# A square root moved ahead of ScalarE's loads, a convolution's first loads moved to GpSimd's queue, and a last store cut in three

## Chip, cores and metric

The kernel runs on one core of a Trainium2 chip. The metric is the device time of one execution in microseconds (us); the time of a kernel is the median of several executions. The engines are named as the profile names them: PE is TensorE, DVE is VectorE, ACT is ScalarE, POOL is GpSimd and SP is SyncE, which here only issues transfers. ACT and POOL issue transfers too, between their computing instructions.

## What is computed

Input `x` is one image of 384 channels and 192 x 192 pixels in float32. Two residual layers follow each other:

```
x = x + attention(gn(x))     # 1x1 conv to q,k,v; 2x2 max pool; 3x3 depthwise conv;
                             # 8 heads of channel attention with four top-k softmaxes;
                             # gelu; 2x2 repeat; 1x1 conv
x = x + conv(gn(x))          # seven depthwise convs (13x13 and six smaller, dilated ones),
                             # each with a batch norm, summed
```

`gn` is a group norm over 32 groups of 12 channels. The seven depthwise convolutions are merged into one of 13 x 13 taps per channel: each set of taps is multiplied by its batch norm's scale, `gamma * rsqrt(var + 1e-5)`, and the sets are added. The batch norms' shifts sum to one value per channel, `shift`.

## The kernel before

Channels stand in 3 tiles of 128 partitions (`NJ` = 3). The kernel has five stages, and within each the order of each engine's instructions is the order in which the Python code issues them (`manual_schedule`), so an engine or a queue that waits holds up all that was issued behind it on the same engine.

**Statistics of x.** Four tiles `xt` (1152 KB each, loaded by SP, line 162) hold the first 16 image rows, and 66 blocks `xs` (768 KB each, line 204) hold the rest. Blocks with an even number are loaded by SP, the others by ACT; ten buffers rotate. `load_block` is called for ten blocks first (lines 207, 208). Then `rsqrt` (lines 86 to 104) computes the scale of the taps: DVE adds eps, ACT takes the square root (line 95), DVE refines it. Lines 210 to 214 make `scale` and `shift` on DVE; POOL scales the taps (lines 216 to 227) and stores them as `wfd`. Behind these on DVE stand 24 `bn_stats` over the `xt` tiles (lines 232, 233) and 198 over the `xs` blocks (line 238), with one `bn_aggr` after each third (line 242). Each pass over a block frees its buffer and so lets the load ten blocks later be issued. `group_stats` (line 106) then turns the channels' mean and variance into those of the groups through tiny matmuls, and the result is `gn0`.

**Projection, pooling and depthwise convolution** (line 339 on PE, 350 and 386 on DVE), then **attention applied to v** (line 709).

**Projection out** (lines 1009 to 1070). A loop over 72 steps, n = 0 to 71, `NBB` = 24 for each channel tile. A step is six matmuls `pj` on PE (line 1018, three of 128 x 128 weights, each executed in two passes), an ACT pass that writes `pjs` (line 1026), a DVE pass that adds the pixel sums `smj` to get `cell` (line 1033), `bn_stats` on DVE (line 1034) and a store of `pjs` to the buffer `pd` in HBM by ACT's queue (line 1036). `load_sum` loads `smj` on SP's queue four steps ahead (line 1005). Three PSUM buffers lie between PE and the two readers. Beside it, generators in the list `running` are advanced once a step:

- `derive(i, ...)` starts at steps 24 and 48 and after the loop. It computes the second group norm's statistics from the channel tiles known so far, through `group_stats`, whose matmuls stand between the steps' matmuls on PE; POOL copies `sv` for it (line 817).
- `load_rows(0)` starts at step 28 (`NBB + 4`) and `load_rows(1)` at step 46. Each loads for the four row phases `u` a piece `raw` of x (line 873) and a piece `up` of `pd` (line 880) on SP's queue, one `u` a step. `load_rows(0)` has ten transfers, `load_rows(1)` eight. `up` can't be loaded before `pd` is stored.
- `load_taps(0)` at step 33 loads 1536 KB of taps `wt` on SP's queue (line 893).
- `residual(0)` on POOL (line 910) from step 37, then at step 44 `patch(0)` on DVE and three passes `normalize1(0, q)` on ACT (line 918), and the transposes `arrange(0, 1)` on DVE (line 933) in two of three steps after it. They prepare the convolution's first chunk.

In the built program every SP or ACT load and store also waits for the transfer eight before it among those of SP and ACT together: their completion is counted on eight shared counters. POOL's transfers have eight counters of their own.

**Convolution** (lines 1081 to 1107). 48 chunks of 8 channels, each 8 times 5 matmuls (line 949), an ACT pass to `co` (line 957), and one chunk later `finish`: one DVE transpose from `co` to `o` (line 963) and four stores to `out`, one for each `u`, by POOL's queue (line 972). `finish` of the last chunk stands alone at the end.

Of the kernel before, what the change touches and what calls it, by code (L numbers as in the profile page):

```python
# [7 lines left out]
F32 = mybir.dt.float32  # L8
AF = mybir.ActivationFunctionType
ALU = mybir.AluOpType  # L10
# [4 lines left out]
P = 128  # L15
C = 384
NJ = C // P
H = W = 192
HW = H * W
# [13 lines left out]
UQ = 4  # L33
# [27 lines left out]
def tile_attn_then_large_kernel_conv(ctx: ExitStack, tc: tile.TileContext, a: dict, out: bass.AP):  # L61
# [43 lines left out]

    def group_stats(pool, psum, mv, name):


        ps = psum.tile([NG, 1], F32, tag="gs", name=f"{name}_ps")
        for j in range(NJ):  # L110
            nc.tensor.matmul(ps, lhsT=gm[:, j, :], rhs=mv[:, j, 0:1], start=(j == 0), stop=(j == NJ - 1))  # L111
        mean = pool.tile([NG, 1], F32, name=f"{name}_mean")
        nc.vector.tensor_copy(mean, ps)
        yield
        yield

        pb = psum.tile([P, NJ, 1], F32, tag="gs", name=f"{name}_pb")
        for j in range(NJ):
            nc.tensor.matmul(pb[:, j], lhsT=gmt[:, j * P : (j + 1) * P], rhs=mean, start=True, stop=True)
        s = pool.tile([P, NJ, 1], F32, name=f"{name}_s")  # L120
        nc.vector.tensor_sub(s, mv[:, :, 0:1], pb)
        nc.vector.tensor_mul(s, s, s)
        nc.vector.tensor_add(s, s, mv[:, :, 1:2])
        yield
        yield
        pv = psum.tile([NG, 1], F32, tag="gs", name=f"{name}_pv")
        for j in range(NJ):
            nc.tensor.matmul(pv, lhsT=gm[:, j, :], rhs=s[:, j], start=(j == 0), stop=(j == NJ - 1))
        var = pool.tile([NG, 1], F32, name=f"{name}_var")
        nc.vector.tensor_copy(var, pv)  # L130
        r = rsqrt(pool, var, 1e-5, name)
        sb = pool.tile([NG, 2], F32, name=f"{name}_sb")
        nc.vector.tensor_copy(sb[:, 0:1], r)
        nc.vector.scalar_tensor_tensor(sb[:, 1:2], mean, -1.0, r, ALU.mult, ALU.mult)
        yield
        yield
        pc = psum.tile([P, NJ, 2], F32, tag="gs", name=f"{name}_pc")
        for j in range(NJ):
            nc.tensor.matmul(pc[:, j], lhsT=gmt[:, j * P : (j + 1) * P], rhs=sb, start=True, stop=True)
        return pc  # L140
# [29 lines left out]
    with (  # L170
# [35 lines left out]

        for n in range(10):
            load_block(n)
        scale = rsqrt(s1, bn[:, :, 3, :], 1e-5, "bn")
# [3 lines left out]
        nc.vector.tensor_sub(sh, bn[:, :, 1, :], sh)  # L213
        nc.vector.tensor_reduce(shift, sh, AX.X, ALU.add)
        c0 = BC - 1
        for j in range(NJ):
# [34 lines left out]
    with ExitStack() as ctx_v:  # L251
# [537 lines left out]
        def derive(i, stats):  # L789
# [6 lines left out]
            yield  # L796
            pc = yield from group_stats(d1, d_ps, mv1, f"g1_{i}")
            chp = d1.tile([P, NJ, 2], F32, name="chp", tag="chp")
            nc.vector.tensor_copy(chp, pc)

            sd = d1.tile([P, NJ], F32, name="sd", tag="sd")
            nc.vector.reciprocal(sd, chp[:, :, 0])
            mean = d1.tile([P, NJ], F32, name="mean", tag="mean")
            nc.vector.tensor_mul(mean, chp[:, :, 1], sd)
            nc.vector.tensor_sub(mean, shift, mean)
            yield
            j0 = max(0, i - 1)
            nj = i + 1 - j0
            dd = d1.tile([P, KK, nj * 2], F32, name="dd", tag="dd")
            nc.vector.tensor_mul(  # L810
                dd,
                of.unsqueeze(2).to_broadcast([P, KK, nj * 2]),
                chp[:, j0 : i + 1].rearrange("p j s -> p (j s)").unsqueeze(1).to_broadcast([P, KK, nj * 2]),
            )
            sv = d1.tile([P, 2, nj, P], F32, name="sv", tag="sv")
            for q, t in enumerate((mean, sd)):
                nc.gpsimd.tensor_copy(sv[:, q], t[:, j0 : i + 1].unsqueeze(2).to_broadcast([P, nj, P]))
            yield
# [10 lines left out]
            ps = d_ps.tile([P, 2, nj, P], F32, tag="gs", name=f"shp{i}")  # L829
            nc.vector.tensor_copy(par[:, :, j0 : i + 1], pp.rearrange("p k (j s) -> p k j s", s=2))  # L830
            for q in range(2):
                nc.vector.tensor_scalar(
                    edge[:, q, :, j0 : i + 1], par[:, :, j0 : i + 1], inside[:, q : q + 1], None, ALU.mult
                )
# [16 lines left out]

        def load_rows(k):
            raw = raws[k] = rotate("raw", k, max(0, k - 1), [P, ME + 1, W], 3)
# [8 lines left out]
            for u in range(UQ):  # L862
# [9 lines left out]
                for p0, p1, m0, m1 in parts:  # L872
                    nc.sync.dma_start(
                        out=raw[u * 32 + p0 : u * 32 + p1, m0:m1],
                        in_=bass.AP(
                            x.tensor, o + p0 * rows + m0 * UQ * W, [[rows, p1 - p0], [UQ * W, m1 - m0], [1, W]]
                        ),
                    )
                par_u, back = (1, 1) if u < 2 else (0, 0)
                nc.sync.dma_start(  # L880
                    out=up[u * 32 : (u + 1) * 32].rearrange("p m w -> p (m w)"),
# [7 lines left out]

        def load_taps(k):  # L890
            wt = taps[k] = rotate("wt", k, k, [P, CC, ZS], 3)
            j, kk = divmod(k, KK)
            nc.sync.dma_start(out=wt, in_=zds[j][kk * CC : (kk + 1) * CC].rearrange("c p z -> p c z"))

# [63 lines left out]

        def finish(k, co, lo):

            o = lo.tile([P, TE, 2, W], F32, tag="o", name=f"o_{k}")
            at, of = o[:, 0], co[:, :, 0, :]
            nc.vector.transpose(  # L963
                bass.AP(at.tensor, at.offset, [list(at.ap[0]), [2 * W, TE], [BC, NBQ], [W, 2], [1, BC]]),
                bass.AP(
                    of.tensor,
                    of.offset,
                    [list(of.ap[0]), [NBQ, TE], [1, NBQ], [NT * NBQ, CC], [TE * NBQ, NE]],
                ),
            )  # L970
            for u in range(UQ):
                nc.gpsimd.dma_start(  # L972
                    out=bass.AP(
                        out.tensor,
                        out.offset + k * CC * HW + 2 * u * W,
                        [[ME * UQ * W, CC * NE], [BR * W, TE], [1, 2 * W]],
                    ),
                    in_=o[u * 32 : (u + 1) * 32].rearrange("p t y w -> p t (y w)"),
                )

        def all_of(gen):
# [12 lines left out]
        with (  # L994
# [4 lines left out]
            with tc.manual_schedule():  # L999
# [9 lines left out]
                for n in range(NJ * NBB):  # L1009
# [34 lines left out]
                    if n == NBB + 4:  # L1044
                        running.append(load_rows(0))
                    if n == NBB + 9:
                        load_taps(0)
                    if n == NBB + 13:
# [10 lines left out]
                    if n == NBB + 22:  # L1059
                        running.append(load_rows(1))  # L1060
                    if n == 2 * NBB + 12:
# [12 lines left out]
    with (  # L1074
# [5 lines left out]
        with tc.manual_schedule():  # L1080
# [4 lines left out]
            for k in range(NK):  # L1085
# [20 lines left out]
                last = co  # L1106
            finish(NK - 1, last, lo)
    ctx_l1.close()
# [49 lines left out]
```

## Time and profile before

| | |
|---|---|
| median of 5 executions | 3181.41 us (3180.43 to 3183.49) |
| profiled execution: its own time | 3181.41 us |
| its span, from first to last instruction | 3179.3 us |
| around the span | 2.1 us |
| PE busy | 2982.9 us (94%) |
| DVE busy | 2488.9 us (78%) |
| ACT busy | 1228.2 us (39%) |
| POOL busy | 869.0 us (27%) |

| stage | from | to |
|---|---|---|
| statistics of x | 0 | 172.4 |
| projection, pooling, attention | 172.4 | 2065.5 |
| projection out | 2065.5 | 2227.5 |
| convolution | 2227.5 | 3164.9 |
| last transpose and stores | 3164.9 | 3179.3 |

The bounds of the stages are starts of instructions in the timeline, in us from the span's start. A busy share over the whole span says little here, as the stages have different limits.

### The profile page before, as it was taken

The page shows a single profiled execution, that of the slowest core. Times are in us where ns is not written, and L with a number is a line of the kernel's source. Part 1 is how long each engine was busy: PE and PEld are TensorE (multiplying, and loading weights), DVE is VectorE, ACT ScalarE, POOL GpSimd, SP SyncE. Part 2 cuts the span into 40 slices and gives each one's busy share as a digit, 9 for nine tenths or more (in the row PEclk, how much of TensorE's full clock was granted, in tenths as well). Part 3 has the DMA queues.
Part 4 walks back from the last instruction along what each step waited for, and adds up shares of the span by engine and source line. Part 5 has one row for each costly group of instructions (what it writes and reads, how often), then busy time and mean ns, then how long its engine had stood idle before and what let it go on. Part 6 is the DMA issues. An engine that isn't in the chain of part 4 may idle for free.

```text
span 3179.3 us, 31595 instructions
## 1 busy us (share of the span) xinstructions
PE 2982.9 (94%) x10978; PEld 1972.0 (62%) x10978; DVE 2488.9 (78%) x3385; ACT 1228.2 (39%) x2288; POOL 869.0 (27%) x1026
## 2 busy tenths in 40 slices
PE   0089999999999999999999999998999999999998
PEld 0056666666666666665555555555777777777776
DVE  6967887878778787879999998356788777777775
ACT  0034444444444444444444443332333333333332
POOL 3023232332323233222222221001333333333332
PEclk9999999999999999999999999999999999999999
DMA  9924444343444434333333333366999999999984
GB/s 371 385 79 121 121 126 124 109 119 110 118 129 122 118 113 116 113 102 125 100 98 114 112 101 113 117 198 208 256 251 249 239 244 240 243 244 240 242 214 107
DMA packets 277744, 528.65 MB, mean 166 GB/s; under 512 B 22132, under 2 KB 193088, under 8 KB 277584
## 3 DMA queue, kind: packets, MB, share of 16 engines
q1 hardware_dynamic: 208064, 338.72, 39.3%
q0 software_dynamic: 43728, 147.74, 16.8%
q10 hardware_dynamic: 25792, 40.17, 3.4%
q8 instruction: 86, 1.41, 0.2%
q14 instruction: 74, 0.61, 0.1%
HBM read 365.18 MB, written 161.37 MB: 166 GB/s over the span
## 4 chain that ended last, share of the span: by engine, by line
PE 87%; DVE 9%; DMA 2%; issue 0%; ACT 0%; POOL 0%; SPq 0%; ACTq 0%; POOLq 0%; DVEq 0%
PE qkv L339 48%; PE conv L949 29%; PE pj L1018 4%; DVE stats L238 4%; PE av L709 3%; DVE v L386 3%; PE gram L427 2%; PE tr L415 2%; DVE mx L350 1%; DMA xt<-in_x 1%; DMA smj<-sums 0%; DMA up<-pd 0%; DMA wt<-zd 0%; DMA pd<-pjs 0%; DVE stats L232 0%
## 5 line engine op out<-in xcount | busy, mean ns | idle before, releaser
L339 PE MATMUL qkv<-xt,wqk 128*128 128x384 f32 x3456 | 1132.8, 487 | 1.3 <-ACT xt L316 1.3
L949 PE MATMUL conv<-xp,wt 128*128 128x288 f32 x3840 | 933.1, 406 | 1.1 <-ACT co L957 1.1
L339 PEld LDWEIGHTS qkv<-xt,wqk 128*128 128x128 f32 x3456 | 650.4, 190 | 435.8 <-ACT xt L316 2.1
L949 PEld LDWEIGHTS conv<-xp,wt 128*128 128x128 f32 x3840 | 729.0, 190 | 202.7 <-ACT co L957 1.6
L386 DVE SCALAR_TENSOR_TENSOR acc<-pooled,wd,acc 128x384 f32<-128x384 f32 (+2 forms) x1152 | 721.0, 626 | 30.6
L350 DVE TENSOR_REDUCE mx<-qkv 128x192 f32<-128x768 f32 x432 | 412.9, 956 | 252.8 <-PE qkv L339 240.6
L933 DVE STREAM_TRANSPOSE xp<-xn 128x4608 f32<-128x4608 f32 (+1 forms) x107 | 442.0, 4131 | 194.5 <-PE conv L949 175.2
L357 ACT ACTIVATE pooled<-mx,bq 128x192 f32<-128x192 f32 x432 | 196.8, 455 | 963.5 <-DVE mx L350 963.5
L339 PE MATMUL qkv<-xt,wv 128*128 128x384 f32 x1728 | 563.4, 487 | 1.6 <-ACT xt L316 1.1
L339 PEld LDWEIGHTS qkv<-xt,wv 128*128 128x128 f32 x1728 | 325.6, 190 | 234.4 <-ACT xt L316 7.1
L957 ACT ACTIVATE co<-conv,cb 128x288 f32<-128x288 f32 x384 | 191.3, 498 | 604.8 <-PE conv L949 604.7
L386 DVE SCALAR_TENSOR_TENSOR v<-pooled,wd,v 128x384 f32<-128x384 f32 (+2 forms) x576 | 375.6, 652 | 15.2
L316 ACT ACTIVATE xt<-xt,gn 128x768 f32<-128x768 f32 x288 | 284.8, 1013 | 2.9 <-DVE gn L243 2.9
L324 POOL TENSOR_TENSOR sum<-xt 128x192 f32<-128x192 f32 x144 | 94.6, 657 | 699.6 <-ACT xt L316 699.0
L972 POOL DMA_DIRECT2D out<-o x192 | 107.3, 594 | 580.5 <-DVE o L963 527.2
L910 POOL TENSOR_TENSOR raw<-raw,up 128x2496 f32<-128x2496 f32 (+2 forms) x56 | 242.5, 4336 | 40.2 <-DMA up<-pd 25.8
L963 DVE STREAM_TRANSPOSE o<-co 128x2304 f32<-128x2304 f32 x48 | 209.8, 4370 | 20.5 <-ACT co L957 20.5
L455 POOL DMA_DIRECT2D zd<-v x96 | 72.0, 756 | 510.7 <-ACT v L446 510.7
L111 PE MATMUL g_ps<-mv,gm 128*32 128x1 f32 x24 | 2.0, 182 | 164.8 <-DVE mv L242 164.2
L1018 PE MATMUL pj<-v,wp 128*128 128x384 f32 x432 | 148.2, 502 | 6.4 <-DVE cell L1033 5.9
L1018 PEld LDWEIGHTS pj<-v,wp 128*128 128x128 f32 x432 | 83.1, 195 | 64.6 <-DVE cell L1033 8.3
L1033 DVE SCALAR_TENSOR_TENSOR cell<-smj,quarter,pj 128x384 f32<-128x384 f32 x72 | 43.8, 608 | 100.3 <-ACT pjs L1026 83.5
(162 smaller groups left out, 1808.5 us busy)
## 6 DMA issues: line engine op xcount, KB each, us to landing
xt<-in_x SPq DMA_DIRECT2D x96, 1152.0 KB, 5.5
wt<-zd SPq DMA_DIRECT2D x48, 1536.0 KB, 13.5
raw<-in_x SPq DMA_DIRECT2D x188, 312.0 KB, 12.5
out<-o POOLq DMA_DIRECT2D x192, 288.0 KB, 6.0
zd<-v POOLq DMA_DIRECT2D x96, 416.0 KB, 4.9
up<-pd SPq DMA_DIRECT2D x192, 156.0 KB, 11.8
xs<-in_x ACTq DMA_DIRECT2D x33, 768.0 KB, 9.6
xs<-in_x SPq DMA_DIRECT2D x33, 768.0 KB, 10.7
```

The source lines that it names most:

```text
L238: nc.vector.bn_stats(stats[:, j, NS0 + b * (FB // 512) + q, :], xt[:, q * 512 : (q + 1) * 512])
L316: nc.scalar.activation(xt[:, j], xt[:, j], AF.Identity, bias=gn0[:, j, 1:2], scale=gn0[:, j, 0:1])
L339: nc.tensor.matmul(ps[:, r, : 2 * W], lhsT=wq[:, j, mm * P : (mm + 1) * P], rhs=xt[:, j, r * 2 * W : (r + 1) * 2 * W], start=(j == 0), sto ...
L350: nc.vector.tensor_reduce(mx, ps[:, :, : 2 * W].rearrange("p r (y w x) -> p r w y x", y=2, x=2), AX.XY, ALU.max,)
L357: nc.scalar.activation(pool_t[m][:, k : k + SR, 1 : 1 + WS], mx, AF.Identity, bias=bq[:, m : m + 1])
L386: nc.vector.scalar_tensor_tensor(acc[:, :nt], pool_t[m][:, k0 + dy : k0 + dy + nt, dx : dx + WS], wd[:, m, t : t + 1], acc[:, :nt], ALU.mu ...
L910: nc.gpsimd.tensor_add(rv, rv, uv.unsqueeze(2).to_broadcast([P, (m1 - m0) * WS, 2]))
L933: nc.vector.transpose(bass.AP(at.tensor, at.offset, [list(at.ap[0]), [NBQ, n], [1, NBQ], [NQ * NBQ, CC], [ME * NBQ, NE]],), bass.AP(row.te ...
L949: nc.tensor.matmul(ps, lhsT=wt[:, c, o : o + P], rhs=d[:, c, g : g + 2 * NT - 1 : 2, :], start=(g == 0), stop=(g == NGR - 1),)
L957: nc.scalar.activation(co[:, c], ps, AF.Identity, bias=cb[:, cc : cc + 1])
L963: nc.vector.transpose(bass.AP(at.tensor, at.offset, [list(at.ap[0]), [2 * W, TE], [BC, NBQ], [W, 2], [1, BC]]), bass.AP(of.tensor, of.offs ...
L1018: nc.tensor.matmul(ps, lhsT=wp[:, j, i * P : (i + 1) * P], rhs=v[:, j, b * RB : (b + 1) * RB, :].rearrange("p r w -> p (r w)"), start=(j = ...
```

## The change

Four edits:

- The calls of `load_block` for the first ten blocks move from ahead of `rsqrt` to behind line 214. On ACT the square root now stands ahead of its first `xs` load. In the built program POOL's nine clearing passes over the pooling tiles (line 303) move in among the scaling of the taps, and on SP the loads `wqk`, `wv` and `bpj` move back among the `xs` loads.
- `load_rows(0)`, `load_taps(0)` and `load_rows(1)` issue their 19 transfers on POOL's queue instead of SP's. In the built program `load_rows(0)` and `load_rows(1)` stand on POOL ahead of the `sv` copies of `derive(0)` and `derive(1)`, the taps between `sv` and `residual(0)`; SP is left with the `smj` loads alone in that loop.
- `group_stats` takes the channel tiles to work on. `derive(i)` passes `range(i + 1)` instead of all three, so it has one tile's matmuls in each of its four groups for i = 0, two for i = 1, three for i = 2; its later small DVE passes cover only the tiles that are used.
- `finish` of the last chunk works in three pieces of two of the six row groups each: three transposes, and after each one four stores, issued by SP, ACT, POOL and SP.

```diff
-    def group_stats(pool, psum, mv, name):
+    def group_stats(pool, psum, mv, name, js=range(NJ)):
+        own = slice(js[0], js[-1] + 1)
...
-        for j in range(NJ):
+        for j in js:
...
-        for n in range(10):
-            load_block(n)
         scale = rsqrt(s1, bn[:, :, 3, :], 1e-5, "bn")
         nc.vector.tensor_mul(scale, scale, bn[:, :, 0, :])
         sh = s1.tile([P, NJ, 7], F32, name="sh")
         nc.vector.tensor_mul(sh, bn[:, :, 2, :], scale)
         nc.vector.tensor_sub(sh, bn[:, :, 1, :], sh)
         nc.vector.tensor_reduce(shift, sh, AX.X, ALU.add)
+        for n in range(10):
+            load_block(n)
...
-            pc = yield from group_stats(d1, d_ps, mv1, f"g1_{i}")
+            pc = yield from group_stats(d1, d_ps, mv1, f"g1_{i}", range(i + 1))
...
-        def load_rows(k):
+        def load_rows(k, eng=nc.sync):
...
-                    nc.sync.dma_start(
+                    eng.dma_start(
...
-        def load_taps(k):
+        def load_taps(k, eng=nc.sync):
...
-        def finish(k, co, lo):
+        def finish(k, co, lo, n=TE, engines=(nc.gpsimd,)):
             o = lo.tile([P, TE, 2, W], F32, tag="o", name=f"o_{k}")
+            for t0 in range(0, TE, n):
+                at, of = o[:, t0], co[:, :, t0, :]
+                nc.vector.transpose(...)
+                for u in range(UQ):
+                    engines[u % len(engines)].dma_start(...)
...
-                        running.append(load_rows(0))
+                        running.append(load_rows(0, nc.gpsimd))
                     if n == NBB + 9:
-                        load_taps(0)
+                        load_taps(0, nc.gpsimd)
...
-                        running.append(load_rows(1))
+                        running.append(load_rows(1, nc.gpsimd))
...
-            finish(NK - 1, last, lo)
+            finish(NK - 1, last, lo, 2, (nc.sync, nc.scalar, nc.gpsimd, nc.sync))
```

## The prediction

> **What bounds the kernel now.** I read the page first, then the chain of waits by stage, then the timeline and the table by stretches at the three places that the change touches. The page's chain says that PE carries most of the end, with DVE and some DMA between:
>
> ```profile
> span 3179.3 us, 31595 instructions
> PE 87%; DVE 9%; DMA 2%; issue 0%; ACT 0%; POOL 0%; SPq 0%; ACTq 0%; POOLq 0%; DVEq 0%
> ```
>
> The change touches no matmul of PE's two long stages, so what can move lies where PE does not carry: the head, the projection out and the tail.
>
> The head, from the timeline (start, duration, engine, line, operation; in brackets the idle time before and what ended it):
>
> ```profile
> 4.82 0.18 DVE L91 TENSOR_SCALAR bn_ve<-bn 128x21 f32<-128x21 f32 x1 [3.94 <-DMA bn<-in_bn]
> ...
> 27.37 0.22 ACT L95 ACTIVATE bn_sd<-bn_ve 128x21 f32<-128x21 f32 x1
> 27.62 0.29 DVE L97 RECIPROCAL bn_r<-bn_sd 128x21 f32<-128x21 f32 x1 [22.62 <-ACT bn_sd L95]
> ...
> 162.48 2.16 DVE L242 BATCH_NORM_AGGREGATE mv<-stats 128x2 f32<-128x444 f32 x1
> ```
>
> The input of the square root is ready at 5.0 and ACT takes it at 27.4, behind five load issues that last 22.55 us. DVE sits for 22.62 us with all the statistics queued behind the reciprocal. From 29.55, its first statistics, to 164.64 it runs without a gap: PE's group matmuls, then the projection, wait for that. The table by stretches (start:end length, busy time of each engine, granted clock, DMA share, GB/s) shows the second limit:
>
> ```profile
> 25.00:40.00 15.00, 0.00 (x0) 0.00 (x0) 12.10 (x32) 1.50 (x2) 9.74 (x30) 1.00 1.02 413
> 40.00:50.00 10.00, 0.00 (x0) 0.00 (x0) 10.00 (x18) 0.00 (x0) 3.21 (x11) 1.00 0.89 293
> 50.00:150.00 100.00, 0.54 (x4) 0.37 (x4) 99.93 (x165) 0.00 (x0) 0.00 (x0) 1.00 1.02 416
> 150.00:153.10 3.10, 0.00 (x0) 0.00 (x0) 3.10 (x6) 0.00 (x0) 0.00 (x0) 1.00 0.96 393
> 153.10:164.70 11.60, 0.01 (x1) 0.01 (x1) 11.50 (x17) 0.00 (x0) 0.00 (x0) 1.00 0.01 5
> ```
>
> Transfers run at 416 GB/s nearly throughout and end at 153.1, with a dip at 40 to 50 when all ten buffers were full. So DVE can't win its whole 22 us: the loads are next.
>
> The projection out, in the chain:
>
> ```profile
> 2141.07 5.09 DMA pd<-pjs
> 2147.16 7.54 DMA smj<-sums
> 2155.50 9.71 PE pj L1018 x24
> 2166.49 1.90 DMA smj<-sums
> 2187.88 2.23 DMA pd<-pjs
> 2190.17 4.21 DMA smj<-sums
> ```
>
> Loads of `smj` stand behind `raw`, `up` and `wt` on SP's queue, which wait for stores of `pd`; then `cell` is late, the PSUM buffers stay full and PE stops. PE was busy 153.2 of the 162.0 us from 2065.5 to 2227.5.
>
> The tail, in the timeline:
>
> ```profile
> 3164.86 4.31 DVE L963 STREAM_TRANSPOSE o<-co 128x2304 f32<-128x2304 f32 x1 [15.05 <-ACT co L957]
> 3169.46 2.24 POOL L972 DMA_DIRECT2D out<-o x4 [17.12 <-DVE o L963]
> ```
>
> The table by stretches has the packets of these stores at 3170.5 to 3176.2, 207 GB/s, and nothing from there to the end at 3179.3.
>
> **The square root first.** On ACT it now waits only for `bn_ve` (5.0): done at 5.3, and DVE's chain behind it (27.62 to 29.6, 2.0 us) ends at 7.3. The first `xt`, issued at 2.2, lands 5.8 us later, at 8.0, so the cover of that chain is the load itself. ACT's first `xs` goes out at about 5.5 instead of 3.5; four `xt` are in transit meanwhile (DMA share 1.00 from 4 to 10), so I cost it at nothing, and at most 2.0 us. POOL's clearing passes move into its scaling work, which ended at 43 and now ends near 30; its result is next read at 171. `wqk` and `wv` (1.73 MB) go out later, still far ahead of the first matmul.
>
> DVE's own bound: the last `xt` lands by 3.7 + 17.2 = 20.9; the first `xs` by 4.6 + 22.5 = 27.1 (22.5 is the longest of these landings). From there 198 x 0.593 + 3 x 2.16 = 123.9 us, so 151.0. The loads' bound: the bytes are the same, and the dip is gone, (416 - 293) x 10 / 416 = 3.0 us, so they end at 150.1 instead of 153.1. Behind the last landing come one or two blocks (1.78 us each) and the last aggregate, 2.16: 154.0 to 155.8. This is later than 151.0, so the loads decide. The aggregate ended at 164.64: gain 8.8 to 10.6, less 2.0 if ACT's later start counts, and less some 3 us if the two queues, now fed in another order, leave gaps like that of 40 to 50. I take 9.5, and 5 to 10.6 as ends. The group matmuls and the 1893 us that follow just move forward.
>
> A rule of the Trainium skill speaks against this. SBUF — State Buffer, section "SBUF: two separate sides", gives HBM to one core about 358 GB/s and calls HBM almost always the bottleneck. By that the 60 MB of the head could not land before 168 us and the gain would be nothing; the rows above, 416 GB/s over 100 us, contradict it, and I go by them.
>
> **Loads on POOL's queue.** What goes: in 2065.5 to 2227.5 PE was idle 8.8 us, and all but pieces of it hangs on late `smj` (2147 to 2155 alone has 8.4 us for 6 matmuls, which take 2.03 elsewhere). SP is left with `smj`, four steps or 8 us ahead of use, landing in 2.5 us. What is late next: at step 44 ACT has three more passes (3.2 us) and DVE eight (1.7 us), and at step 54 DVE has ten small passes of `derive(1)` beside `cell`, `bn_stats` and a transpose, some 4 us in a step of 2.03. The three PSUM buffers absorb about two steps; I leave 1.5 us of idle time, between 0.5 and 5.
>
> What comes: 19 issues on POOL. The trace has no such load on this queue. The nearest rows are its stores: `zd` in many small pieces 0.76 us an issue and 4.9 to landing, the clearing stores 1.70 and up to 13.0, `out` 0.58 and 6.0. POOL is nearly idle in this stage (11 us of 162), so 19 x 0.76 = 14 us or 19 x 1.70 = 32 us costs POOL nothing. What waits behind: `sv` (step 32, its matmuls some five steps later), then `residual(0)`, whose result ACT needs at step 44, about 2157. The stores of the first tile's `pd` end near 2117.5. Ten transfers, two in turn because the ninth and tenth wait for earlier ones: 2117.5 + 6 + 2 x 6 = 2136 by the small rows, 2117.5 + 12 + 2 x 13 = 2156 by the clearing rows. The taps follow `sv` at 2133 and land at 2141 to 2148. `residual(0)` takes 5.5 us: done at 2142 to 2161. Cost 0, or 4 us at the far end. I take 0, as sizes and pieces are closest to `zd`.
>
> [...]
>
> **Fewer group matmuls.** These stand on PE between the steps. The four groups of `derive(0)` took 0.28, 0.75, 0.28 and 0.76 us; two thirds go: 1.4. Of `derive(1)` one third: 0.7. The small DVE passes shrink from 3 columns to 1 or 2; 128x3 takes 0.16 and 32x1 0.15, so nothing. Together 2.1 us, if PE carries the stage, which it does.
>
> The stage: 8.8 - 1.5 + 2.1 = 9.4 us gained; ends 2 (5 us of idle time and 4 late rows, with only part of the rest) and 10.9. The start of the convolution (a wait for `wt` and `up` of later chunks, PE idle 1.2 us) keeps its loads on SP and I leave it.
>
> **The tail.** Three transposes of 768 elements, 4.31 / 3 = 1.44 each: ready at 3166.3, 3167.8, 3169.2. The last piece is 0.39 MB instead of 1.18. POOL's first packets came 1.04 us after its issue started, so at 3170.5 as before; 0.39 MB at 207 GB/s is 1.9 us, so packets end at 3172.4, and with the same 3.1 us after them the span ends at 3175.5: gain 3.8. If the earlier pieces' 0.79 MB from 3167.4 on is still in the way, 3173.1: gain 3.1. At the 416 GB/s of the head: 4.8.
>
> **The sum**, against the profiled execution, 3181.41, of which 2.1 lie around the span; it equals the median: 9.5 + 9.4 + 3.8 = 22.7, so 3158.7.
>
> **Rivals.**
> The first: in the head the loads' new order leaves gaps, or two queues with eight transfers in flight don't hold 416 GB/s from the start. For it: 324 GB/s in the first 25 us. Against: 413 as soon as ten blocks are queued. Gain 4 instead of 9.5: 3164.2.
> The second: the projection out stays short of PE's pace, because DVE's work around steps 44 to 60 was as much the cause as `smj`. For it: 2.1 us of PE's idle time is put down to `dd` on DVE. Against: DVE was behind there because of `smj`. Gain 3 instead of 9.4: 3165.1. Both together: 3170.6.
> The third ends slower: `raw`, `up` or `wt` come so late through POOL's queue that `patch(0)` and `normalize1(0)`, issued at step 44, hold up every later `cell` and `pjs` behind them on DVE and ACT. It decides once they are over 22.7 us later than 2157; at 45 us late, 3181.4 - 22.7 + 45 = 3203.7. Against: it takes landings of over 20 us, where this queue's longest is 13.0.
> That an edit does nothing is not open: the built order has each of them.
>
> **How the numbers follow.** All three gains, 0.72: 3158.7, by the ends of the terms 3154 to 3165. First rival 0.08, second 0.12, both 0.03, third 0.03; 0.02 for what I don't see. The range that leaves out 2 in 10 at most runs from 3154 (10.6 + 10.9 + 4.8 = 26.3 gives 3155.1, and a microsecond of spread) to 3168. Runs of this kernel lie within 0.1% of their median, so about 0.2%, 6.4 us, can be told from no change: faster 0.94, the same 0.03, slower 0.03.
>
> **What would show it.** Right: `bn_sd` on ACT near 5; the first statistics near 8; gaps on DVE between `xs` blocks, ended by DMA; the last aggregate at 154 to 157; DMA near 416 from 25 to 150. `smj` not in the chain; PE busy 151 of about 152.6 us in the projection out; POOL's load issues under 1 us. Three transposes of 1.4 us and the end 6 us behind the last. Wrong: an aggregate later than 160, PE waits for `cell` or ACT's `xn` after step 44, `raw` on POOL waiting for DMA past 2150 (less the head's gain), or packets in the tail past 3173.

## The result, and the profile after

The changed kernel takes 3174.57 us (median of 21 executions, 3171.07 to 3176.21); the kernel before, run beside it, takes 3180.97 us (41 executions, 3178.34 to 3184.44). The ratio is 0.9978, with a 95% interval of 0.9972 to 0.9984: faster by 6.4 us. The forecast was 3158.7 us, 22.7 us faster, with a range from 3154 to 3168. The sign was right; the size was not, and the time lies outside the range.

The profiled execution took 3172.44 us, 2.1 us less than its median. In its page's chain of waits PE has 86% instead of 87%, DVE 8% instead of 9%, and DMA 4% instead of 2%.

Stage by stage, in us, each stage bounded by the starts of the same instructions in both timelines:

| stage | forecast gain | before | after | gain |
|---|---|---|---|---|
| statistics of x, to the first `qkv` | 9.5 | 172.37 | 167.07 | 5.3 |
| projection, pooling, attention, to the first `pj` | 0 | 1893.11 | 1892.79 | 0.3 |
| projection out, to the first `conv` | 9.4 | 162.05 | 160.71 | 1.3 |
| convolution, to the last transpose | 0 | 937.33 | 938.19 | -0.9 |
| last transpose to the end of the span | 3.8 | 14.4 | 11.8 | 2.6 |

Before rounding the gains add up to the 8.7 us by which the span is shorter. All three terms are gains, and two of them are smaller than forecast, by some 4 and 8 us. The 1.3 us of the projection out are less than the 2 us by which this stage differs between executions (see the experiments).

**The head**, in the timeline (start, duration, engine, line, operation; in brackets the idle time before it and what ended it):

```profile
5.17 0.22 ACT L95 ACTIVATE bn_sd<-bn_ve 128x21 f32<-128x21 f32 x1 [1.37 <-DVE bn_ve L91]
...
7.90 0.69 DVE L233 BATCH_NORM_STATS2 stats<-xt 128x6 f32<-128x512 f32 x1 [0.47 <-DMA xt<-in_x]
...
70.64 1.88 DVE L239 BATCH_NORM_STATS2 stats<-xs 128x6 f32<-128x512 f32 x3 [5.14 <-DMA xs<-in_x]
...
157.17 2.16 DVE L243 BATCH_NORM_AGGREGATE mv<-stats 128x2 f32<-128x444 f32 x1
```

The square root ran at 5.17 instead of 27.37 and the first statistics at 7.90 instead of 29.55, as forecast. But DVE, which ran without a gap before, now stands still for 5.14 us in the middle of the loads, and the last aggregate ends at 159.33 instead of 164.64. The table by stretches (start:end length, busy time of each engine, granted clock, DMA share, GB/s) shows that the DMA did not stand still with it:

```profile
40.00:50.00 10.00, 0.00 (x0) 0.00 (x0) 9.10 (x16) 0.00 (x0) 0.00 (x0) 1.00 1.02 417
...
65.00:71.00 6.00, 0.00 (x0) 0.00 (x0) 0.86 (x2) 0.00 (x0) 0.00 (x0) 1.00 1.02 415
71.00:150.00 79.00, 0.54 (x4) 0.36 (x4) 78.80 (x129) 0.00 (x0) 0.00 (x0) 1.00 1.02 414
150.00:153.00 3.00, 0.00 (x0) 0.00 (x0) 3.00 (x7) 0.00 (x0) 0.00 (x0) 1.00 0.12 49
```

The dip of 40 to 50 us is gone (417 GB/s instead of 293), the transfers end near 150 as forecast, and at 65 to 71 they run at 415 GB/s while DVE has 0.86 us of work in 6. What they carry there is in the chain of waits (start, duration, what):

```profile
33.33 17.18 DMA xs<-in_x
...
50.52 18.22 DMA wqk<-in_wqkvT
...
68.81 14.86 DMA xs<-in_x
```

The weights `wqk` and `wv` (1152 and 576 KB) were issued at 29.00 and 29.42 before, when DVE was behind and the buffers were full:

```profile
29.00 0.38 SPq L272 DMA_DIRECT2D wqk<-in_wqkvT  x1
```

They are issued at 50.52 and 58.52 now, among the blocks that DVE is waiting for; and the `xs` load that shares its counter with `wqk` is not issued before `wqk` has landed, at 68.8.

**The projection out**, in the table of waits between 2059 and 2221 (who waited for whom: us in total, times, longest):

```profile
ACT pjs L1030 <- DMA pd<-pjs: 15.8, 5, 5.5
...
PE pp L823 <- DVE dd L812: 2.8, 1, 2.8
...
DVE cell L1037 <- DMA smj<-sums: 2.8, 2, 1.5
```

The same table of the kernel before, between 2065.5 and 2227.5, has

```profile
DVE cell L1033 <- DMA smj<-sums: 16.6, 6, 5.1
...
ACT pjs L1026 <- DMA pd<-pjs: 4.7, 2, 2.8
```

`smj`, which `cell` waited 16.6 us for, is down to 2.8 us. In its place ACT waits 15.8 us, where it waited 4.7, for stores of its own: `pjs` has three buffers, and a store of `pd` that is late leaves ACT without one. The chain of this stage has the two late stores, and a third piece that is new:

```profile
2113.37 8.04 DMA pd<-pjs
...
2130.71 5.27 DVE dd L812
...
2166.81 12.60 DMA pd<-pjs
```

The time from issue to landing of the stores of `pd`, where the trace has the landing, in the kernel before and in the changed one:

```profile
DMA to landing us min/median/max: 2.0/2.1/7.4
...
DMA to landing us min/median/max: 2.0/2.1/12.6
```

Each of the two late ones was issued within a burst of eight loads on POOL (2109.88 to 2114.4 and 2162.98 to 2167.7), which issues them at about 0.6 us each as soon as nothing holds it. The timeline of POOL and DVE:

```profile
2109.88 0.52 POOL L882 DMA_DIRECT2D up<-pd  x1 [158.33 <-DMA pd<-pjs]
...
2130.58 5.39 DVE L812 TENSOR_TENSOR dd<-of,chp 128x32 f32<-128x32 f32 x1
2130.95 5.46 POOL L912 TENSOR_TENSOR raw<-raw,up 128x576 f32<-128x576 f32 x5
```

The last two rows belong to the piece with `dd`. This DVE pass of `derive(0)` took 0.17 us in the kernel before and takes 5.39 us here, beside the five adds of `residual(0)` on POOL; it ends at 2135.97, just behind the fourth add (2135.91). PE waits 2.8 us for the `dd` that feeds its `pp`. The `dd` of `derive(1)` starts 0.2 us behind the first add of `residual(1)` and takes 1.14 us in both kernels: it waits for that one add.

**The tail**, in the timeline:

```profile
3158.76 4.42 DVE L967 STREAM_TRANSPOSE o<-co 128x768 f32<-128x768 f32 x3 [15.05 <-ACT co L959]
```

Three transposes as forecast, with the stores of each behind it on three engines; the last packets move at 3166.2, 7.4 us behind the start of the transposes, where the forecast had 7.5. The end of the span comes another 4.4 us later, where it had 3.1.

### The profile page after: what moved, and what is told of

The parts are those of the page before. It is cut to its first block, busy times and chain, and to the rows that moved or that the text cites. A ratio compares the mean times of both kernels' runs of the same rounds, so it can differ in the third digit from the quotient of the medians.

```text
span 3170.6 us, 31552 instructions
## 1 busy us (share of the span) xinstructions
PE 2979.6 (94%) x10954; PEld 1969.4 (62%) x10954; DVE 2498.3 (79%) x3387; ACT 1228.1 (39%) x2288; POOL 878.4 (28%) x1044
## 4 chain that ended last, share of the span: by engine, by line
PE 86%; DVE 8%; DMA 4%; issue 1%; POOL 0%; ACT 0%; SPq 0%; DVEq 0%; POOLq 0%; ACTq 0%
PE qkv L340 48%; PE conv L951 28%; PE av L710 3%; PE pj L1022 3%; DVE v L387 3%; DVE stats L239 2%; PE gram L428 2%; PE tr L416 2%; DVE mx L351 1%; DMA xs<-in_x 1%; DMA xt<-in_x 1%; DMA pd<-pjs 1%; DMA wqk<-in_wqkvT 1%; DMA raw<-in_x 1%; DVE cell L1037 0%
## 5 line engine op out<-in xcount | busy, mean ns | idle before, releaser
L967 DVE STREAM_TRANSPOSE o<-co 128x2304 f32<-128x2304 f32 (+1 forms) x50 | 209.9, 4202 | 20.5 <-ACT co L959 20.5
L1022 PE MATMUL pj<-v,wp 128*128 128x384 f32 x432 | 146.2, 498 | 2.5 <-DVE cell L1037 1.9
L239 DVE BATCH_NORM_STATS2 stats<-xs 128x6 f32<-128x512 f32 x198 | 118.4, 677 | 6.6 <-DMA xs<-in_x 5.9
## 6 DMA issues: line engine op xcount, KB each, us to landing
wt<-zd SPq DMA_DIRECT2D x47, 1536.0 KB, 12.6
raw<-in_x SPq DMA_DIRECT2D x182, 312.0 KB, 12.5
xs<-in_x ACTq DMA_DIRECT2D x33, 768.0 KB, 12.1
```

The lines of the kernel that those rows point to most:

```text
L239: nc.vector.bn_stats(stats[:, j, NS0 + b * (FB // 512) + q, :], xt[:, q * 512 : (q + 1) * 512])
L967: nc.vector.transpose(bass.AP(at.tensor, at.offset, [list(at.ap[0]), [2 * W, n], [BC, NBQ], [W, 2], [1, BC]]), bass.AP(of.tensor, of.offse ...
L1022: nc.tensor.matmul(ps, lhsT=wp[:, j, i * P : (i + 1) * P], rhs=v[:, j, b * RB : (b + 1) * RB, :].rearrange("p r w -> p (r w)"), start=(j = ...
```

## The experiments

The theory after the comparison: (1) the head lost what the moved weights take, since from 28 us on DVE takes a block in 1.88 us on average, the aggregates counted in (123.9 us for 66 blocks), and the loads bring one in 1.89 (768 KB at 416 GB/s), so that DVE never makes up a gap; (2) the projection out lost its gain to stores of `pd` that land late beside POOL's loads and to too few buffers behind them, and to `dd` beside POOL's adds. The rivals: in the head, that two queues simply go less well together; in the projection out, that PE's matmuls or DVE were the bound anyway, so that the queue had nothing to give. All ratios are to the kernel before, run beside each, with 95% intervals; differences to the changed kernel are between medians of separate runs, and by the ratios they come out the same within 2 us. Stages of one execution vary: kernels with the same code in the projection out (before, the square root alone, the tail alone) had 162.05, 162.18 and 164.23 us there, so differences of 2 us in one profile mean nothing.

### Each edit alone

**The square root alone**, on the kernel before:

```diff
-        for n in range(10):
-            load_block(n)
         scale = rsqrt(s1, bn[:, :, 3, :], 1e-5, "bn")
...
+        for n in range(10):
+            load_block(n)
```

> The kernel before with the first edit alone: the ten calls of load_block behind the square root. If the head of the changed kernel is this edit's work alone, the last aggregate ends at 159.3 as there (164.6 before), with DVE waiting 5 us near 65 to 71 behind the load of wqk, and the time falls by 5.3 us (ratio 0.9983). If the trace's head was only a lucky execution, the time falls by less than 3 us (ratio above 0.999).

3175.46 us, ratio 0.9980 [0.9971, 0.9989]. PE starts `qkv` at 166.91, against 167.07 with all edits. The gap on DVE, in the timeline, is there to the tenth:

```profile
70.57 3.66 DVE L238 BATCH_NORM_STATS2 stats<-xs 128x6 f32<-128x512 f32 x6 [5.20 <-DMA xs<-in_x]
```

So the whole gain of the head is this edit's, and its shortfall too.

**POOL's queue alone**, on the kernel before:

```diff
-                        running.append(load_rows(0))
+                        running.append(load_rows(0, nc.gpsimd))
-                        load_taps(0)
+                        load_taps(0, nc.gpsimd)
-                        running.append(load_rows(1))
+                        running.append(load_rows(1, nc.gpsimd))
```

> The kernel before with the second edit alone: load_rows(0), load_taps(0) and load_rows(1) on POOL's queue. Theory: POOL has nothing that paces it, issues the transfers in one burst, the stores of pd land after 8 us and more instead of 2, ACT runs out of its three pjs buffers and PE stops; the projection out gains 0 to 2 us of its 8.8 us of idle time (ratio 0.9994 to 1.0003). Rival, the prediction's reading: smj was the cause, and the stage gains 7 us (ratio 0.9978).

3185.14 us, ratio 1.0012 [1.0003, 1.0021]: slower by 3.8 us, which is worse than expected; 1.1 us of it lie in the tail, from the start of the last transposes to the end (15.5 us instead of 14.4). The stage takes 162.21 us. The table of waits of this stage has the same exchange as the full change:

```profile
ACT pjs L1026 <- DMA pd<-pjs: 17.0, 5, 5.5
...
DVE cell L1033 <- DMA smj<-sums: 3.6, 2, 1.8
```

Stores of `pd` take up to 13.4 us and `dd` takes 4.87. The wait for `smj` is gone and the stage is no shorter.

**Fewer group matmuls alone** (the edits of `group_stats` and `derive`):

```diff
-            pc = yield from group_stats(d1, d_ps, mv1, f"g1_{i}")
+            pc = yield from group_stats(d1, d_ps, mv1, f"g1_{i}", range(i + 1))
```

> The kernel before with the third edit alone: group_stats over the first i + 1 channel tiles. If PE's matmuls carry the projection out, 2.1 us less (ratio 0.9993). If waits of ACT and DVE set its pace around these matmuls, less than 1 us (0.9997 to 1).

3181.65 us, ratio 0.9997 [0.9988, 1.0006]. Inconclusive: the interval reaches from a gain of 3.8 us to a loss of 1.9 and so holds the 2.1 that was forecast as well as nothing. The stage was 159.85 us in this one profile. In its timeline the groups of tiny matmuls in this stage take 3.1 us on PE instead of 4.9, so 1.7 of the 2.1 us did go from PE's work; whether the kernel's time fell by as much does not show.

**The tail alone:**

```diff
-            finish(NK - 1, last, lo)
+            finish(NK - 1, last, lo, 2, (nc.sync, nc.scalar, nc.gpsimd, nc.sync))
```

> The kernel before with the last edit alone: the last chunk finished in three pieces by three engines. If the tail stands by itself, from the start of the last transpose to the end of the span 11.8 us instead of 14.4, so 2.6 us less (ratio 0.9992). By the prediction's sum 3.8 us less (0.9988).

3177.40 us, ratio 0.9989 [0.9980, 0.9998]. From the start of the last transposes to the end of the span it takes 10.5 us instead of 14.4: a gain of 3.9 in the profile (3.8 was forecast) and 3.9 between the medians. In the full change the same stores end 1.3 us later.

By the medians the four edits alone are worth 5.9, -3.8, -0.3 and 3.9 us, in the order above, together 5.7; the whole change is worth 6.4.

### The head: where the weights are loaded

**Behind the last block.** `wqk` and `wv` get tiles of their own, and SP loads them behind the last `xs`:

```diff
+    wqp = ctx_x.enter_context(tc.tile_pool(name="wqp", bufs=1, side="right"))
...
             if b == NX - 1:
                 nc.vector.bn_aggr(...)
+        wqk = wqp.tile([P, NJ, 2 * C], F32, name="wqk")
+        wv = wqp.tile([P, NJ, C], F32, name="wv")
+        wqkv = a["wqkvT"].rearrange("(j p) o -> p j o", p=P)
+        nc.sync.dma_start(out=wqk, in_=wqkv[:, :, : 2 * C])
+        nc.sync.dma_start(out=wv, in_=wqkv[:, :, 2 * C :])
```

> The changed kernel with wqk and wv loaded by SP behind the last xs block (in tiles of their own; nothing else moved). Theory: the move of these 1.73 MB among the xs loads starved DVE near 65 to 71; without it DVE runs nearly without gaps from 28, and the last aggregate ends at 152 to 154 instead of 159.3; the weights land before PE starts. About 6 us less than the changed kernel, ratio to before 0.996. Rival: DVE must wait for x anyway, as x at 416 GB/s lasts to 146 and DVE is never ahead of it; aggregate at 157 to 159, ratio 0.998.

3169.10 us, ratio 0.9958 [0.9945, 0.9970]. PE starts `qkv` at 162.59, 4.5 us earlier than in the changed kernel. In the timeline DVE has two short gaps left, and the last aggregate ends at 154.87, a little later than the 152 to 154 expected:

```profile
42.58 22.41 DVE L240 BATCH_NORM_STATS2 stats<-xs 128x6 f32<-128x512 f32 x36 [0.31 <-DMA xs<-in_x]
65.44 3.66 DVE L240 BATCH_NORM_STATS2 stats<-xs 128x6 f32<-128x512 f32 x6 [0.45 <-DMA xs<-in_x]
...
152.71 2.16 DVE L244 BATCH_NORM_AGGREGATE mv<-stats 128x2 f32<-128x444 f32 x1
```

The 4.5 us are about what the two loads weigh: 1728 KB at 416 GB/s are 4.25 us.

**Behind the tenth block.** The same tiles and loads, right behind the first ten calls of `load_block`, ahead of the loads that wait for buffers:

```diff
         for n in range(10):
             load_block(n)
+        wqk = wqp.tile([P, NJ, 2 * C], F32, name="wqk")
...
+        nc.sync.dma_start(out=wqk, in_=wqkv[:, :, : 2 * C])
+        nc.sync.dma_start(out=wv, in_=wqkv[:, :, 2 * C :])
```

> The changed kernel with wqk and wv loaded by SP right behind the first ten xs blocks, where the kernel before had them. If it is the place among the transfers that wait in turn, the loads all end at 150 and DVE waits for them in small pieces: last aggregate 154 to 156, 4 us less than the changed kernel. If any place ahead of the last xs starves DVE by the same, 159, no less.

3174.77 us, ratio 0.9979 [0.9970, 0.9988]: no gain over the changed kernel. The second of the two expected cases came: the last aggregate ends at 160.96. The gap on DVE is earlier and no smaller, in the timeline:

```profile
54.52 21.45 DVE L245 BATCH_NORM_STATS2 stats<-xs 128x6 f32<-128x512 f32 x36 [6.75 <-DMA xs<-in_x]
```

PE starts `qkv` at 168.68. At both places ahead of the last block the weights keep DVE waiting once, for at least as long as their bytes take, and DVE has no pace to spare to get it back. This run alone does not part the bytes from the shared counter, for SP waits here too for `wqk` before it issues its next `xs` load (6.6 us in SP's table of waits). The DMA does: it moves 409 GB/s while DVE stands still here (47.7 to 54.5) and 415 in the changed kernel, so the wait for the counter left no gap in the transfers, and what DVE waits out is the bytes.

### The projection out: buffers, queue, pace

**Eight buffers for `pjs`** instead of three, on the changed kernel:

```diff
-                    pj = by.tile([P, 2, RB // 2, WS], F32, tag="pjs", name="pjs")
+                    pj = by.tile([P, 2, RB // 2, WS], F32, tag="pjs", name="pjs", bufs=8)
```

> The changed kernel with eight pjs buffers instead of three. Theory: ACT stops because the stores of pd land late in POOL's burst and hold the three buffers; with eight the stores may be late and ACT goes on. The projection out falls from 160.7 us to 155, with dd on DVE (5.4 us beside POOL's residual) still there; 5 us less than the changed kernel. Rival: the eight shared completion counters hold ACT's stores on their queue all the same, or smj lands late too, and less than 2 us go.

3160.43 us, ratio 0.9932 [0.9918, 0.9945], 14.1 us less than the changed kernel, where 5 were expected. The stage takes 148.46 us instead of 160.71; `dd` now comes ahead of POOL's adds and takes 0.17 us. No wait of ACT for a store of `pd` is left in its table of waits, though the stores still take up to 12.5 us; the row of `pj` and the stage in the table by stretches:

```profile
2060.80:2209.30 148.50, 146.15 (x473) 85.45 (x474) 100.70 (x212) 48.10 (x79) 22.34 (x31) 1.00 0.73 216
```

PE is busy 146.15 of 148.50 us at a granted clock of 1.00. The same row of the changed kernel:

```profile
2059.90:2220.60 160.70, 150.19 (x473) 86.80 (x474) 106.00 (x212) 48.03 (x79) 22.33 (x31) 0.98 0.69 200
```

It has the same 473 matmuls in 150.19 us, at a clock of 0.98: in two stretches, 3.4 us each from 2126.4 and 2136.7, the granted clock is 0.5.

**Eight buffers on the kernel before**, the same edit, loads still on SP:

> The kernel before with eight pjs buffers and nothing else, loads on SP's queue as they were. The prediction's reading of the kernel before: PE stops there because smj stands behind raw, up and wt on SP's queue; then eight pjs buffers change little, the projection out stays at 160 to 162 us (ratio 0.999 to 1). Rival: late stores of pd held ACT there as well, and the stage falls to 155 or less (ratio 0.9975 or less).

3182.53 us, ratio 0.9998 [0.9989, 1.0007]: no difference. The stage takes 160.11 us, and in its table of waits `cell` waits for `smj` as in the kernel before, while ACT's waits for `pd` are 1.8 us:

```profile
DVE cell L1033 <- DMA smj<-sums: 14.5, 6, 4.3
```

So the forecast's reading of the kernel before was right: there `smj` on SP's queue was the cause, and buffers alone give nothing.

**The residual step by step.** On the changed kernel, POOL copies one element of the previous step's `bn_stats` ahead of each of the five adds of `residual(0)` and of `residual(1)`, so that no add runs ahead of its step:

```diff
+                if n == 3:
+                    pacer[0]()
                 rv = raws[k][:, m0:m1].rearrange("p m (w x) -> p (m w) x", x=2)
...
+                def pace():
+                    i, b = divmod(pace_at[0], NBB)
+                    nc.gpsimd.tensor_copy(pace_t, stats1[:, i, b, 0:1])
```

> The changed kernel with each piece of residual(0) and residual(1) on POOL held to its step, by a one-element POOL copy of the bn_stats of the step before. Theory: dd on DVE took 5.4 us instead of 0.2 because POOL's residual ran at that moment; apart from it dd takes 0.2 us, PE loses its wait of 2.9 us for it, and the projection out falls by 2 to 4 us. Rival: dd was long for another reason (the DMA burst), stays over 2 us, and nothing falls.

3171.19 us, ratio 0.9967 [0.9954, 0.9979], 3.4 us less than the changed kernel, but the two intervals overlap, so in the kernel's time this is not clear of noise. `dd` takes 0.17 to 0.21 us, 7 us and more ahead of the adds, and PE no longer waits for it; the stage of this execution takes 156.98 us, 3.7 less. ACT's waits for stores stay:

```profile
ACT pjs L1042 <- DMA pd<-pjs: 23.0, 7, 5.3
```

So the long `dd` came from the adds beside it, and it is a loss apart from the stores, the smaller of the two.

**The loads step by step as well**, with three buffers: POOL takes the same one-element copy ahead of each `u` of `load_rows`, so that a burst of eight or ten loads becomes one `u` a step.

```diff
             for u in range(UQ):
+                if eng is nc.gpsimd:
+                    pacer[0]()
```

> The changed kernel, three pjs buffers, with POOL's loads held to one u per step and residual's pieces held to their steps, each by a one-element POOL copy of the bn_stats of the step before. Theory: the burst makes the stores of pd late; with the loads spread over four steps each no store lands after more than 5 us, ACT's waits for pd (16 to 23 us in the runs with the burst) fall under 5 us and the projection out ends at 150 to 153 us, near the 148.5 of eight buffers (ratio 0.994). Rival: the same bytes in the same place make the stores late even when paced; 156 us as with residual alone, ratio 0.9965.

3174.54 us, ratio 0.9972 [0.9962, 0.9982]: the same as the changed kernel. The stage takes 162.48 us, longer than in either expected case. The chain still has two late stores:

```profile
2127.08 10.77 DMA pd<-pjs
...
2172.23 11.31 DMA pd<-pjs
```

My idea that the burst does it fell for the second store: spread over four steps, the loads of `load_rows(1)` still delay it to 11.31 us (12.60 in the burst). The first store says less: the taps, one transfer of 1536 KB that is not spread, go out here at 2128.99, 1.9 us behind it. Two stores that fall among the spread loads of `load_rows(0)` take 5.1 and 5.6 us, against 8.0 and 8.5 in the burst. PE's longest waits here, 5.6 us for `par` and 4.7 for `g_sb`, stand in the chain right behind the two late stores.

### The two remedies together, and what the queue is worth

**The changed kernel with the weights behind the last block and eight buffers.** The edits are those of the weights behind the last block and of eight buffers, shown above:

```diff
+        nc.sync.dma_start(out=wqk, in_=wqkv[:, :, : 2 * C])
+        nc.sync.dma_start(out=wv, in_=wqkv[:, :, 2 * C :])
...
+                    pj = by.tile([P, 2, RB // 2, WS], F32, tag="pjs", name="pjs", bufs=8)
```

> The changed kernel with the weights behind the last xs block and eight pjs buffers. If the two effects add, 4.5 us less in the head and 12 us less in the projection out than the changed kernel: 3154 to 3157, ratio 0.9918.

3156.78 us (3156.11 to 3157.04), ratio 0.9917 [0.9904, 0.9931]. PE starts `qkv` at 163.66, and the projection out takes 148.16 us. This is 26.5 us less than the kernel before, run beside it; the change was forecast to bring 22.7.

**The same, with the 19 loads left on SP:**

```diff
-                        running.append(load_rows(0, nc.gpsimd))
+                        running.append(load_rows(0))
-                        load_taps(0, nc.gpsimd)
+                        load_taps(0)
-                        running.append(load_rows(1, nc.gpsimd))
+                        running.append(load_rows(1))
```

> The same as the one with both additions, but with load_rows and load_taps left on SP's queue. If the move to POOL's queue is worth something once the stores have buffers, the projection out is longer here by the waits of cell for smj, 5 us or more (ratio 0.9935). If the buffers alone were what was missing, the same time as with POOL's queue (0.992).

3165.88 us, ratio 0.9950 [0.9938, 0.9963]. The stage takes 159.74 us, and `smj` is the wait again:

```profile
DVE cell L1038 <- DMA smj<-sums: 15.2, 5, 4.7
```

With eight buffers POOL's queue is worth 11.6 us in the stage and 9.1 between the medians. With three it was worth nothing, and eight buffers without it were worth nothing either: the two waits cover each other, and the stage gets shorter only when both go.

## Why the prediction was right or wrong

**The head, 9.5 forecast, 5.3 measured: right about the square root and the loads, wrong about DVE's end.** The square root, DVE's start, the end of the dip, 416 GB/s and the end of the loads near 150 came as forecast. The step that failed is "DVE's own bound": 124 us of work from 27.1 on, done at 151.0, "so the loads decide". It set DVE's work against the end of the loads, as if DVE were always free to work ahead, and let `wqk` and `wv` go out later at no cost. But from 28 us on DVE and the loads run at one pace, so DVE's end is its start plus its work plus every gap. The two gaps of the loads' stretch (0.79 and 5.14) put 151.9 (27.96 + 123.9) at 157.8; it ended at 159.33, as smaller waits at other blocks add the rest. The loads had ended some 7 us earlier, so they did not decide. Before, the weights had come while DVE was behind with all buffers full, and were free. The forecast's lower end, 5, was meant for gaps of the queues; that is what held 5.3, though the gap's cause was another one, shown by the run with the weights behind the last block. That the bound held was luck. The first rival (4 for this term) came near the size as well, by gaps in the transfers, and there were none: in the changed kernel they ran at 408 GB/s or more in every stretch from 25 to 150.

A figure of the Trainium skill that the prediction went against, SBUF — State Buffer, section "SBUF: two separate sides", of about 358 GB/s from HBM to one core, does not hold here either: 414 GB/s over 79 us in the changed kernel. The section's figure is half of what two cores share; here one core runs.

**The projection out, 9.4 forecast, 1.3 measured: wrong.** Three steps of it were right. `smj` was the cause in the kernel before; POOL's issues took 0.51 to 0.94 us, and `residual(0)` was done at 2136.4, ahead of need. The step that failed is "What is late next". It went through ACT's and DVE's passes and the loads on POOL, and not through the third queue: the stores of `pd` on ACT's queue, with three buffers behind them, and 4.7 us of waits for them in the trace of before already. The loads of POOL's queue delayed them to 12.6 us, and that wait took the place of the one that was removed. The price put on the move itself was wrong the same way: "19 issues on POOL" were counted by what they cost POOL and by when they land, not by what their bytes cost others. The second rival came nearer in size (3 for this term) but by another mechanism, DVE's work around steps 44 to 60. With eight buffers that work hid within steps, so it is refuted.

A smaller miss stands in the same step: `residual(0)` was weighed only by when it is done, not by what its adds cost others. It moved beside `dd`, and `dd` took 5.39 us. The same section of SBUF — State Buffer says that a DVE pass with two SBUF inputs and a GpSimd instruction that reads SBUF take a shared port in turn, each for its whole length. The runs agree in kind: 4.29 to 5.39 us in the four kernels where the first `dd` fell beside the five adds, 1.04 to 1.16 where the second one started behind the first of five adds, and 0.17 to 0.21 where a `dd` came ahead of them (eight buffers, and the residual step by step). But the wait need not end with one instruction of GpSimd: the first `dd` was held to the end of the fourth add, the second to that of the first, and why they differ is open.

Two figures of the term were off without moving its result: with the 0.5 us of idle time that the forecast calls the least, its upper end is 10.4 and not 10.9, and the last store of the first tile's `pd` landed at 2114.8 in the trace of before, not near 2117.5.

The floor was wrong too, on the other side. The forecast took PE's 153.2 busy us, less 2.1, as what the stage could not go below. With the stores out of the way PE needed 146.15. Its busy time had grown with its waits: 502 ns for a `pj` in the kernel before, at a mean clock of 0.97, and 488 in the kernel with eight buffers, at 1.00. By the table by stretches the granted clock of the kernel before was 0.5 for 3.4 us three times in this stage (from 2149.4, 2156.2 and 2200.6), each time within 1.3 us of the end of a wait of PE. The prediction's own 2.03 us a step times 72 gives 146.2 and would have shown it.

**Fewer group matmuls, 2.1 forecast:** 1.7 us less work on PE; a gain in time is neither shown nor refuted, as it is within the interval of its own run.

**The tail, 3.8 forecast, 2.6 measured.** The edit is worth what was forecast: 3.9 alone. The other 1.3 us come from the loads on POOL's queue. The two pairs of kernels that differ in that alone end 14.4 and 15.5 us behind the start of the last transposes (before, and with POOL's queue), and 10.5 and 11.8 (the two last kernels). The forecast had no such term.

**The convolution, nothing forecast, 0.9 lost:** PE waits there 2.0 us instead of 1.1; no experiment was made on it. The seven other kernels with POOL's queue have 937.4 to 937.8 us there, so most of the loss belongs to this one execution.

**The sum.** Of the 22.7 us, 4.2 are missing in the head, 8.1 in the projection out, 1.2 in the tail and 0.9 in the convolution, against 0.3 won between head and projection out. That leaves 8.6 of the 9.0 that the profiled execution gained (the rest lies around the span); its median is 2.1 above it, and the median of before 0.4 lower than the 3181.41 that the sum began with: 6.4. The three gains together were given 0.72; "both together", at 3170.6, was given 0.03, and it was the nearest case. The two shortfalls were priced as rivals of each other, though each had a reason of its own, and the bounds of the terms were added up only for the case where all went well: their lower ends, 5, 2 and 3.1, give 3171.3, which the range left out.

## What to carry to other kernels

When loads leave a queue, follow their bytes as well as their place: ask which stores of a third queue will be late beside them, and how many buffers these stores have. A wait that is removed and a wait that it covered must go together. Where a consumer and its loads run at the same pace, as here, a gap is not made up, so what is not needed yet is loaded behind the last block; look in the order of the built program for all transfers that an edit moves, not only for those that it names. The floor of this stage was its step times its number of steps, 146.2 us, and not PE's busy time of 153.2, which had grown with PE's waits.

## What the runs showed of the hardware

- Stores of 192 KB on ACT's queue took 2.1 us in the median and up to 12.6 while POOL's queue loaded a megabyte or more (12.1 to 13.4 in the seven other kernels with these loads), and at most 7.4 in the kernel before, with the same loads on SP (7.3 to 8.2 in the five others with the loads there). By the table by stretches the DMA share was 0.87 in the changed kernel from 2110 to 2140. How the 16 engines share between queues was not tried; spread over four steps, the second tile's loads still delayed a store to 11.3 us.
- The worth of POOL's queue, 9.1 us with eight buffers, is that of waits on SP's queue. The Trainium skill, DMA: Bandwidth & Descriptors, section "Issuing engines are not separate DMA queues", says that issuing from several engines saves the sequencer's time alone, usually little beside the transfer. Here it was more, since the instructions of SP wait in their order.
- A DVE pass of 0.17 us waited through four POOL adds in a row (5.39 us); a like pass, started behind the first of five, waited for one (1.14 us).
- The granted clock was 0.5 for 3.4 us at a time, three times in the kernel before and twice in the changed one, each time within 1.3 us of the end of a wait of PE of 1.9 to 2.9 us, and 1.00 throughout the stage with eight buffers and POOL's queue.
- Of the two pairs, the kernels with the loads on POOL's queue end 1.1 and 1.3 us later in the tail than those without, and have one packet of an instruction queue in the last 10 us that the others lack. That POOL's longer program is fetched there is a guess from this; it was not tried by itself.
